# Attention with a token branch on one core: the tokens' second softmax product moved behind the next sample's y and V's first two blocks, its division moved behind the turning of the maximum

## The chip, the cores and the metric

The kernel runs on one core of one Trainium2 chip. The metric is the device time of one execution in microseconds. The kernel before takes 914.13 us, the median of three runs (914.01 to 916.65). All data are fp32.

A core has a matrix engine, TensorE (PE in the profile, with its weight loads shown apart as PEld), VectorE (DVE), ScalarE (ACT), GpSimd (POOL) and SyncE (SP), which issues most of the transfers here. Each engine runs its own list of instructions in order, and the lists meet at semaphores. Matmuls write to PSUM, a memory of eight banks, from which ScalarE and VectorE copy or add the results into SBUF.

## The reference

16 samples, each with 100 queries of width 640 and a context of 722 rows of width 384. The last 4 context rows are the "tokens" (`ca`), the other 718 are ordinary keys and values. 8 heads of width 80.

```python
query = hidden_states @ Wq
keyt = enc @ Wk
valt = enc @ Wv
hs = _mha(query, keyt, valt)                       # 100 queries on 718 keys
ca_q1 = jnp.einsum('btc,th->bch', ca, Wq_ca)
ca_q1 = ca_q1[:, indices, :]                       # 100 rows picked
ca_hs1 = _mha(ca_q1, residual, residual)           # the tokens' first attention, over x
ca_q2 = ca_hs1 @ Wq
ca_k2 = ca @ Wk_ca
ca_v2 = ca @ Wv_ca
ca_hs2 = _mha(ca_q2, ca_k2, ca_v2)                 # the tokens' second attention, 4 keys
out = (hs + ca_hs2) @ Wout + b_out + residual
```

## The kernel before

**The loop.** One pass of the loop `for b in range(B)` (L1410 on) handles sample b, and at the same time prepares sample b + 1. The order of the work is written out by hand: every engine executes its instructions in the order in which the program issues them. Samples 0 to 14 go through the branch `if b + 1 < B`; sample 15, the last, has a branch of its own.

In a pass, TensorE computes the scores of sample b in three parts (`scores(b, 0..2, ...)`, L688). Each part ends or begins with products of a 32-row shape (`others`) and of a 64-row shape (`heads`); the third part ends with the 32-row shape. ScalarE copies them to SBUF (L719, L725). VectorE keeps the running maximum in `most` (`larger(i)`, two element-wise maxima of about 1 us each, L1440). When all three parts are in, the class `Maximum` brings the maximum over the keys to every partition in steps: `top.go(1)` issues the first (a transpose, "turned", L760), the next reduces ("quad", L762), the next reduces again ("side" and "mx", L765 and L772), then it is spread and transposed back. After that the scores are reduced by it (`subtract`), exponentiated on ScalarE and multiplied with V (r_ps L1579 and a_ps L1597).

**The tokens' branch.** For sample b, `Second` makes `y` and `g` from x and a small matrix `m2` (`products()`: ten matmuls y_ps, L836, and a reduction g on VectorE, L845; `copy()`: ScalarE's copy of y out of PSUM into the one buffer `y_there`, L857). GpSimd then makes first scores `e1` out of g (`scores1`, L871 and L878); they pass a maximum and an exponential. In the next pass `softmax2()` multiplies the exponentials with y: 64 small matmuls with 32 output columns each into the bank z_ps (L898). One column of z_ps is the softmax's sum, so VectorE takes its reciprocal (L907) and multiplies (L909). `scores2()`, `softmax3()`, `spread2()` and `values2()` take it from there.

**V and K.** V of sample b and K of sample b + 1 are computed with 15 block products each (`V_PLAN`, `K_PLAN`), called by `vv.go(n)` and `kk.go(n)`, which issue the next n blocks. A V block is two accumulating targets of 320 columns, a K block two of 240. The letters A to E name the PSUM banks: the first blocks of V's plan are A, B, D, and K's too. A block's result is copied by ScalarE if it is the first for its place in the output (L418), else added by VectorE (L416).

**PSUM.** There are three pools: `ps2`, two pairs of banks (the third score part, then V's A and B); `psk`, two banks (K's A and B); and `ps1`, two single banks, of which y_ps, z_ps, V's D, E, C (one bank for each half) and K's D, E, C take turns. A new tile takes the bank that was let go first, and its first matmul waits until the last reader of the tile before is done with it.

So at the place of the change TensorE's order in samples 0 to 14 is: the third score part, z of sample b, y of sample b + 1, then V's A, B, D and K's A, B, D, and `scores2()` goes to the other engines behind that. In the pool `ps1` the takers are in turn z, y, V's D (two halves), K's D.

Of the kernel before, what the change touches and what calls it, by code (L numbers as in the profile page):

```python
# [14 lines left out]
B, S, H = 16, 100, 640  # L15
NH, D = 8, 80
# [26 lines left out]
HT = NH * T  # L43
# [44 lines left out]
def load_outputs(load, to, w):  # L88

    rows = w.rearrange("(c e k) n -> e c k n", e=2, k=D)  # L90
    for e in range(2):
        load(
            out=to[64 * e : 64 * e + 64, : HC - 1],
            in_=rows[e, :, FIRST[e] : FIRST[e] + 64].rearrange("c k n -> k c n"),
        )
        for c in range(HC - 1):
            at = 32 * c + 16 * e
            load(
                out=to[at : at + 16, HC - 1],
                in_=rows[e, c, 64:] if e == 0 else rows[e, c, : FIRST[1]],  # L100
            )
# [46 lines left out]
def kernel(  # L148
# [343 lines left out]
    def enc_sums(enc, part=slice(None)):  # L492

        at = lambda f: a_form(enc, f)
        raw = lambda u, c: a_raw(enc, u - 1, c - 1)
        sums = (
            (at(7), raw(2, 3), raw(3, 1), ALU.add),
            (at(11), raw(3, 2), raw(3, 3), ALU.add),
            (at(8), at(11), raw(2, 3), ALU.subtract),
            (at(10), raw(1, 3), at(11), ALU.subtract),  # L500
            (at(9), raw(2, 1), raw(2, 2), ALU.add),
            (at(2), raw(1, 1), at(9), ALU.subtract),
            (at(9), at(9), raw(3, 1), ALU.subtract),
            (at(5), raw(1, 1), raw(2, 1), ALU.subtract),
            (at(5), at(5), raw(2, 3), ALU.add),
            (at(11), raw(1, 3), raw(3, 3), ALU.subtract),
            (at(11), at(11), raw(3, 1), ALU.add),
            (at(4), at(2), at(10), ALU.add),
            (at(4), at(4), raw(1, 2), ALU.add),
        )  # L510
        begun = None
        for out, left, right, op in sums[part]:
            first = nc.gpsimd.tensor_tensor(out, left, right, op)  # L513
            begun = begun or first
        return begun
# [217 lines left out]
    def wait_for(ins, other):  # L733

        tc.add_manual_dep(
            ins.ins,
            other.ins.name,
            mybir.DependencyInfo(
                mybir.DependencyClass.Sync, mybir.DependencyReason.DATA
            ),  # L740
            reason="apart",
        )
# [49 lines left out]
    def load_m(b, behind=None):  # L792
        if b < 2:
            return lambda c: m_sb[c][:, b * HT : (b + 1) * HT]
        mb = small.tile([P, HC, HT], F32, tag="mb", name=f"mb_{b}")
        loaded = nc.sync.dma_start(
            out=mb, in_=m_d[:, :, b * HT : (b + 1) * HT].rearrange("c p n -> p c n")
        )
        if behind:
            wait_for(loaded, behind)  # L800
        return lambda c: mb[:, c]
# [13 lines left out]
    class Second:  # L815
# [77 lines left out]
        def softmax2(self):  # L893
            b = self.b
            z_ps = (psum1 if b + 1 < B else psumk)(f"z_ps_{b}")
            for h in range(NH):
                for lo, hi in QZ:
                    nc.tensor.matmul(  # L898
                        z_ps[lo:hi, h * (HT + 1) : (h + 1) * (HT + 1)],
                        e1[:S, h * S + lo : h * S + hi],  # L900
                        self.y[:, h, :],
                        start=True,
                        stop=True,
                    )
            z_v = z_ps[:S, : NH * (HT + 1)].rearrange("p (h k) -> p h k", h=NH)
            rz = small.tile([S, NH], F32, tag="rz", name=f"rz_{b}")
            nc.vector.reciprocal(rz.unsqueeze(2), z_v[:, :, HT:])  # L907
            z = small.tile([S, NH, HT], F32, tag="z", name=f"z_{b}")
            nc.vector.tensor_tensor(  # L909
                z, z_v[:, :, :HT], rz.unsqueeze(2).to_broadcast([S, NH, HT]), ALU.mult  # L910
            )
            self.z = z
# [88 lines left out]
    def again():  # L1001

        rows = wout.rearrange("(c e k) n -> e c k n", e=2, k=D)
        for e in range(2):
            nc.sync.dma_start(
                out=w_there[0][1][64 * e : 64 * e + 64],
                in_=rows[e, :2, FIRST[e] : FIRST[e] + 64, H // 2 :].rearrange(
                    "c k n -> k c n"
                ),
            )  # L1010
# [4 lines left out]
    def store(behind):  # L1015
        while held:
            r, xn = held.pop(0)
            lo, n = OC[r]
            stored = nc.sync.dma_start(
                out=out.rearrange("b s n -> (b s) n")[lo : lo + n], in_=xn[:n]  # L1020
            )
            wait_for(stored, behind)
# [367 lines left out]
    for c in range(HC):  # L1390
        for half in range(2):
            h = 2 * c + half
# [17 lines left out]
    for b in range(B):  # L1410
        p = b // 2
        e_in, now = enc, second
# [25 lines left out]
        def larger(i):  # L1438
            for u in range(2):
                most_now = nc.vector.tensor_tensor(  # L1440
                    most[:KN], most[:KN], st[i][:, u], ALU.max
                )
            return most_now
# [12 lines left out]
        vv = Values(b, e_in, V_PLAN if b + 1 < B else END_PLAN)  # L1456
        if b + 1 < B:
            kk = Keys(b + 1, enc)
        now.softmax2()
        if b + 1 < B:  # L1460
            second.products()
            second.copy()
        seen = larger(2)
        top = Maximum(most, f"{b}", True)

        if b + 1 < B:

            def both(n):
                vv.go(n)
                kk.go(n)  # L1470

            if waiting:
                wait_for(enc_sums(enc, LATE_SUMS), seen)
            if waiting:
                second.scores1(tokens=range(T - 1))
            else:
                second.scores1(seen)
            store(seen)
            if last:
                last.load(seen)  # L1480
            if b == B - 2:
                again()
            if b + 2 < B:
                m_next = load_m(b + 2, seen)
            if b == 1:
                load_outputs(nc.sync.dma_start, wout_sb, wout)
            top.go(3)
            both(3)
            now.scores2()
            top.go(1)  # L1490
            both(2)
            top.go()
            both(2)
            now.softmax3()
            if waiting:
                second.scores1(tokens=range(T - 1, T))
            if b + 2 < B:
                keys(m_next)
            both(1)
            now.spread2()  # L1500
            vv.go(2)
            kk.go(1)
            subtract(0)
            exponential(0)
            vv.go(1)
            less = subtract(1)
            if last:
                last.place(less)
                if last.b in PAIRED:
                    last.row_sums()  # L1510
                last.add_bias()
            if b == B - 2:
                mine.load(seen)
            now.values2()
            if b == B - 2:
                mine.add_bias()
            vv.go(1)
            kk.go(2)
            exponential(1)
            vv.go(1)  # L1520
            kk.go(2)
            both(1)
            both(1)
            if b == 1:
                nc.gpsimd.dma_start(out=bias, in_=bout[0].partition_broadcast(P))
            second_next, enc_next = loads()
            subtract(2)
            exponential(2)
            last_keys(b + 1, enc, b in (6, 7))
            if b + 2 < B:  # L1530
                enc_next = load_rest(b + 2, enc_next)
        else:
            last.place()
            mine.load(seen)
            top.go(3)
            vv.go(3)
            top.go(1)
            now.scores2()
            last.project_few(len(OC) - 2)
            last.project((0,), True, put=False)  # L1540
            top.go()
            now.softmax3()
            vv.go(1)
            now.spread2()
            vv.go(1)
            less = subtract(0)
            exponential(0)
            wait_for(subtract(2, nc.gpsimd), less)
            subtract(1, nc.gpsimd)
            mine.add_bias()  # L1550
            now.values2()
            vv.go(5)
            exponential(2)
            vv.go(1)
            exponential(1)
            vv.go(4)
            last.put()
# [109 lines left out]
```

## Time and profile before

| | |
|---|---|
| median of three runs | 914.13 us |
| the profiled execution, by the same clock as the runs | 915.1 us |
| its span, first to last instruction in the profile | 913.4 us |
| TensorE busy | 907.1 us, 99% |
| VectorE busy | 668.5 us, 73% |
| GpSimd busy | 619.4 us, 68% |
| ScalarE busy | 375.2 us, 41% |
| granted TensorE clock | 1.000 |

How to read the rows that follow: in the engine shares each engine has its busy time, its share of the span and the number of its instructions. A row of the waits names the waiting engine and line, what it waited for, the total in us, how often, and the longest. "issue" means that the profile shows nothing that was waited for. A row of the timeline begins with the start (us from the span's start) and the duration, then engine, line, operation, out<-in, the shape and the number of instructions that were merged; brackets give the engine's idle time ahead of it and what ended it. Matmuls overlap in the array: the start of a block and the start of the next one tell more than the duration.

### The profile page before, as it was taken

How to read it: one execution, taken by the hardware profiler on the slowest of the kernel's cores; microseconds unless marked ns; L12 is line 12 of the kernel's file. 1: busy time of each engine (PE TensorE's matmuls, PEld its weight loads, DVE VectorE, ACT ScalarE, POOL GpSimd, SP SyncE). 2: the span in 40 equal slices, each digit the busy share in tenths (PEclk: the TensorE clock that was granted, in tenths of full speed). 3: DMA queues.
4: the chain of work that ended last, by engine and by line, in shares of the span. 5: the costliest groups of instructions: out<-in, count | busy, mean ns of one | idle time of the engine just before them, and what ended most of it. 6: DMA issues, size and time to landing. Idle time of an engine off the chain costs nothing.

```text
span 913.4 us, 26025 instructions
## 1 busy us (share of the span) xinstructions
PE 907.1 (99%) x11127; PEld 758.2 (83%) x11127; DVE 668.5 (73%) x1121; ACT 375.2 (41%) x649; POOL 619.4 (68%) x653
## 2 busy tenths in 40 slices
PE   9999999999999999999999999999999999999998
PEld 7988889787887879878788888988888888887865
DVE  4899795979649796676957769588782888828773
ACT  1354534444334453443434434344541445424451
POOL 9664786677847788476674756755796567955635
PEclk9999999999999999999999999999999999999999
DMA  8604351141302303140221402304140151401313
GB/s 275 231 13 134 61 126 37 25 124 40 103 12 71 107 21 95 44 133 12 69 76 44 133 12 70 82 7 135 43 111 11 35 140 37 111 11 45 86 34 83
DMA packets 68060, 69.48 MB, mean 76 GB/s; under 512 B 25193, under 2 KB 61353, under 8 KB 67945
## 3 DMA queue, kind: packets, MB, share of 16 engines
q1 hardware_dynamic: 67016, 66.97, 27.1%
q8 instruction: 87, 1.43, 0.7%
q10 hardware_dynamic: 464, 0.52, 0.2%
q0 software_dynamic: 464, 0.34, 0.2%
q14 instruction: 29, 0.23, 0.1%
HBM read 62.14 MB, written 8.94 MB: 78 GB/s over the span
## 4 chain that ended last, share of the span: by engine, by line
PE 98%; POOL 1%; ACT 0%; DVE 0%; issue 0%; DVEq 0%; POOLq 0%
PE s_ps L688 12%; PE v_psA L445 11%; PE v_psB L445 9%; PE k_psA L476 8%; PE a_ps L1597 7%; PE q_ps L550 7%; PE k_psB L476 7%; PE kT_ps L601 5%; PE r_ps L1579 4%; PE v_psC L445 4%; PE kT_ps L576 3%; PE k_psC L476 3%; PE y_ps L836 2%; PE v_psD L445 2%; PE v_psE L445 2%; PE o_psy L1165 2%
## 5 line engine op out<-in xcount | busy, mean ns | idle before, releaser
L871 POOL TENSOR_TENSOR e<-ca,g 100x800 f32<-100x800 f32 x60 | 91.7, 1539 | 96.9 <-DVE most L1440 74.5
L445 PE MATMUL v_psA<-wv_sb,enc 128*120 128x320 f32 x384 | 119.5, 434 | 0.0
L513 POOL TENSOR_TENSOR enc<-enc 128x240 f32<-128x240 f32 x144 | 110.0, 773 | 8.0
L445 PE MATMUL v_psB<-wv_sb,enc 128*120 128x320 f32 x320 | 99.2, 432 | 0.0
L878 POOL TENSOR_TENSOR e<-e,e 100x800 f32<-100x800 f32 x45 | 92.2, 2048 | 3.5
L445 PEld LDWEIGHTS v_psA<-wv_sb,enc 128*120 128x120 f32 x384 | 69.0, 183 | 24.7 <-DVE vs L416 0.9
L1428 DVE TENSOR_TENSOR st<-st,over 120x1600 f32<-120x1600 f32 x46 | 88.7, 1929 | 0.0
L476 PE MATMUL k_psA<-enc,wk_sb 128*128 128x240 f32 x360 | 87.6, 366 | 0.0
L476 PEld LDWEIGHTS k_psA<-enc,wk_sb 128*128 128x128 f32 x360 | 68.4, 190 | 17.1
L445 PEld LDWEIGHTS v_psB<-wv_sb,enc 128*120 128x120 f32 x320 | 58.6, 183 | 23.4
L1436 ACT ACTIVATE st<-st 120x1600 f32<-120x1600 f32 x48 | 73.9, 1539 | 8.0 <-DVE st L1428 5.5
L1440 DVE TENSOR_TENSOR most<-most,st 120x800 f32<-120x800 f32 x64 | 63.5, 993 | 16.3 <-ACT st L719 15.1
L688 PE MATMUL s_ps<-qp,kT 64*56 64x100 f32 (+1 forms) x3072 | 73.5, 248 | 0.1
L476 PE MATMUL k_psB<-enc,wk_sb 128*128 128x240 f32 x300 | 73.0, 366 | 0.0
L688 PEld LDWEIGHTS s_ps<-qp,kT 64*64 64x64 f32 (+1 forms) x3072 | 67.0, 130 | 6.1 <-issue 4.2
L1449 DVE TENSOR_TENSOR most<-st 120x800 f32<-120x800 f32 x16 | 17.4, 1090 | 73.8 <-ACT st L725 73.8
L1597 PE MATMUL a_ps<-st,vs 120*64 120x100 f32 (+1 forms) x1536 | 69.5, 250 | 0.0
L550 PE MATMUL q_ps<-xT,wq_sb 128*128 128x200 f32 x400 | 69.1, 332 | 0.0
L1597 PEld LDWEIGHTS a_ps<-st,vs 120*64 120x64 f32 (+1 forms) x1536 | 66.4, 137 | 2.7 <-issue 2.7
L550 PEld LDWEIGHTS q_ps<-xT,wq_sb 128*128 128x128 f32 x400 | 68.0, 190 | 0.2
L418 ACT COPY vs<-v_psA 120x640 f32<-120x640 f32 x48 | 33.2, 692 | 83.7 <-PE v_psA L445 83.7
L725 ACT COPY st<-s_ps 120x800 f32<-120x800 f32 x64 | 49.7, 829 | 43.2 <-PE s_ps L688 43.1
(187 smaller groups left out, 1874.7 us busy)
## 6 DMA issues: line engine op xcount, KB each, us to landing
pb<-p_d SPq DMA_DIRECT2D x32, 400.0 KB
enc<-in_enct SPq DMA_DIRECT2D x30, 240.0 KB
enc<-in_enct SPq DMA_DIRECT2D x15, 360.0 KB
xT<-in_xt SPq DMA_DIRECT2D x8, 500.0 KB
rest<-in_enct SPq DMA_DIRECT2D x31, 120.0 KB
xn<-in_x SPq DMA_DIRECT2D x11, 320.0 KB
wide_d<-p_d SPq DMA_DIRECT2D x16, 200.0 KB
pb<-wide_d SPq DMA_DIRECT2D x16, 200.0 KB
```

The source lines that it names most:

```text
L445: nc.tensor.matmul(at[0][j][:KN, : H // 2], a_form(self.enc, f)[:, j * KN : (j + 1) * KN], wv_sb[:, W_AT[f]], start=first, stop=last, skip ...
L476: nc.tensor.matmul(at[:, i * KT : (i + 1) * KT], wk_sb[:, W_AT[f], i], a_form(self.enc, f), start=(first and i == 0), stop=last, skip_grou ...
L513: first = nc.gpsimd.tensor_tensor(out, left, right, op)
L550: nc.tensor.matmul(q_ps[:, : 2 * S].rearrange("p (j s) -> p j s", j=2), wq_sb[:, c, n * P : (n + 1) * P], xT[:, :, c, :], start=(c == 0), ...
L688: nc.tensor.matmul(s_ps[bank][keys, 256 * a + lo : 256 * a + lo + rhs.shape[-1]], kT[rows, c, u, j * KN + keys.start : j * KN + keys.stop] ...
L725: nc.scalar.copy(st[:, :, 4 * i * S : 4 * (i + 1) * S].rearrange("p a (r q) -> p r a q", r=2), pairs[i][:n].rearrange("p r (a q) -> p r a ...
L871: first = engine.tensor_tensor(to, self.ca[:, t, :].unsqueeze(1).to_broadcast([S, NH, S]), g[:, :, t].unsqueeze(2).to_broadcast([S, NH, S] ...
L878: engine.tensor_tensor(e, e, to, ALU.add)
L1428: return engine.tensor_tensor(st[i], st[i], top.over[:KN].unsqueeze(1).to_broadcast([KN, 2, ROWS]), ALU.subtract,)
L1436: nc.scalar.activation(st[i], st[i], AF.Exp, scale=SCALE)
L1440: most_now = nc.vector.tensor_tensor(most[:KN], most[:KN], st[i][:, u], ALU.max)
L1597: nc.tensor.matmul(wides[64 * e : 64 * e + 64, h // 2], slot(i, h, FIRST[e], 64), st[i // 2][: KEYS[i], i % 2, PLACE[h] * S : (PLACE[h] + ...
```

## The change

In samples 0 to 14 the product of `softmax2()` (z) is issued behind the next sample's `products()` (y) and the first two blocks of V (A and B), where it was issued ahead of them. ScalarE's copy of y is issued behind z, as z still reads the old y out of the one buffer. The reciprocal and the multiplication by it become a method of their own, `divide2()`, issued on VectorE behind the last `larger(2)` and behind the first step of the maximum (the turning); before they stood ahead of `larger(2)`. The blocks that followed are issued as K's A and B, then V's D, then K's D. In sample 15 `divide2()` follows `softmax2()` directly, which is the order of before.

```diff
                         start=True,
                         stop=True,
                     )
-            z_v = z_ps[:S, : NH * (HT + 1)].rearrange("p (h k) -> p h k", h=NH)
+            self.z_ps = z_ps
+
+        def divide2(self):
+            b = self.b
+            z_v = self.z_ps[:S, : NH * (HT + 1)].rearrange("p (h k) -> p h k", h=NH)
             rz = small.tile([S, NH], F32, tag="rz", name=f"rz_{b}")
             nc.vector.reciprocal(rz.unsqueeze(2), z_v[:, :, HT:])
...
         if b + 1 < B:
             kk = Keys(b + 1, enc)
-        now.softmax2()
         if b + 1 < B:
             second.products()
+            vv.go(2)
+            now.softmax2()
             second.copy()
+        else:
+            now.softmax2()
+            now.divide2()
         seen = larger(2)
         top = Maximum(most, f"{b}", True)
...
-            top.go(3)
-            both(3)
+            top.go(1)
+            now.divide2()
+            top.go(2)
+            kk.go(2)
+            vv.go(1)
+            kk.go(1)
             now.scores2()
             top.go(1)
             both(2)
```

`both(n)` stands for `vv.go(n)` followed by `kk.go(n)`.

## The prediction

> **What bounds the kernel now.** I read the page's engine shares first, then the chain that ended last, then the waits of TensorE's weight loads, and last the timeline around the moved product.
>
> ```profile
> PE 907.1 (99%) x11127; PEld 758.2 (83%) x11127; DVE 668.5 (73%) x1121; ACT 375.2 (41%) x649; POOL 619.4 (68%) x653
> ...
> PE 98%; POOL 1%; ACT 0%; DVE 0%; issue 0%; DVEq 0%; POOLq 0%
> ...
> PEld r_ps L1579 <- issue: 5.0, 15, 0.4
> PEld s_ps L688 <- issue: 4.2, 17, 0.3
> PEld z_ps L898 <- issue: 3.9, 15, 0.5
> ...
> PEld z_ps L898 <- ACT e L891: 0.4, 1, 0.4
> ```
>
> TensorE (PE) is busy for 907.1 of 913.4 us and makes 98% of the chain. So a microsecond on another engine is worth nothing unless it makes a matmul wait, and a microsecond in which TensorE waits is lost at full price. The matmuls stay the same in number and shape. What can change is the time between them. The last four rows are the weight loads' idle time: almost all of it stands at "issue", with no data named, and z, the product that is moved, has 3.9 us of it in 15 of its 16 instances.
>
> The edit acts in samples 0 to 14. In sample 15 the product and its division follow each other as before. This is the stretch of sample 2 (start, duration; x counts the instructions):
>
> ```profile
> 157.20 0.95 PE L688 MATMUL s_ps<-qz,kT 32*120 32x200 f32 x16
> 158.08 0.75 PE L898 MATMUL z_ps<-y,e 100*32 100x33 f32 x64
> 158.76 1.21 PE L836 MATMUL y_ps<-m,xT 128*100 128x96 f32 x10
> 159.80 1.26 PE L445 MATMUL v_psA<-wv_sb,enc 128*120 128x320 f32 x4
> 160.90 1.24 PE L445 MATMUL v_psB<-wv_sb,enc 128*120 128x320 f32 x4
> 161.98 1.24 PE L445 MATMUL v_psD<-wv_sb,enc 128*120 128x320 f32 x4
> 163.05 0.97 PE L476 MATMUL k_psA<-enc,wk_sb 128*128 128x240 f32 x4
> 163.86 0.97 PE L476 MATMUL k_psB<-enc,wk_sb 128*128 128x240 f32 x4
> 164.67 0.97 PE L476 MATMUL k_psD<-enc,wk_sb 128*128 128x240 f32 x4
> ```
>
> From start to start: z 0.68, y 1.04, vA 1.10, vB, vD 1.08 each, a K block 0.81. TensorE waits for none of them. The new order is y, vA, vB, z, kA, kB, vD, kD.
>
> **The change part by part.** *The start of y in z's place.* The scores' last products (32-row shape) are followed by 0.24 us of idle weight loads before z:
>
> ```profile
> 158.08 0.64 PEld L898 LDWEIGHTS z_ps<-y,e 100*32 100x32 f32 x64 [0.24 <-issue]
> ...
> 191.86 2.05 PEld L1579 LDWEIGHTS r_ps<-st,vs 120*32 120x32 f32 x96 [0.30 <-issue]
> ...
> 189.34 0.57 PE L601 MATMUL kT_ps<-rest,wk 128*128 128x240 f32 x2
> 189.74 1.78 PE L601 MATMUL kT_ps<-enc,wk 128*128 128x240 f32 x8
> 191.36 0.57 PE L601 MATMUL kT_ps<-rest,wk 128*128 128x240 f32 x2
> 191.86 2.27 PE L1579 MATMUL r_ps<-st,vs 120*32 120x100 f32 x96
> ```
>
> Such idle time stands wherever the tile shape changes, here too before r (0.30), whose operands were long there. So y will find it as z did, and starts at 158.08. If it did not, it could win 0.24 at most, and the next step takes that away again.
>
> *vA moves up by z's 0.68 us.* It writes the pair of banks from which ScalarE (ACT) copies the last scores:
>
> ```profile
> L725 ACT COPY st<-s_ps 120x800 f32<-120x800 f32 x64 | 49.7, 829 | 43.2 <-PE s_ps L688 43.1
> ...
> 158.24 1.55 ACT L725 COPY st<-s_ps 120x800 f32<-120x800 f32 x2 [0.91 <-PE s_ps L688]
> ...
> 162.77 0.91 ACT L418 COPY vs<-v_psD 120x320 f32<-120x320 f32 x2
> 164.06 0.56 ACT L418 COPY kT<-k_psA 128x480 f32<-128x480 f32 x1 [0.39 <-PE k_psA L476]
> 164.87 0.56 ACT L418 COPY kT<-k_psB 128x480 f32<-128x480 f32 x1 [0.25 <-PE k_psB L476]
> ```
>
> The first row is their group on the page: a copy takes 829 ns on average, and two overlap a little: the first pair is free near 159.07, the second at 159.79. vA would come at 158.08 + 1.04 = 159.12. With some 0.05 us for a semaphore (the k_psE rows below) it can go at about 159.12 to 159.20: between 0 and 0.08 us lost, I take 0.03 as the copy is all but done. vB follows at 160.25, long after the second copy. If vA has the second pair, it waits to 159.84, 0.7 us per sample. I put that aside because in another sample the copies ran later and vA did not:
>
> ```profile
> 599.18 1.55 ACT L725 COPY st<-s_ps 120x800 f32<-120x800 f32 x2 [1.19 <-PE s_ps L688]
> ...
> 600.46 1.26 PE L445 MATMUL v_psA<-wv_sb,enc 128*120 128x320 f32 x4
> ```
>
> There the second copy ended at 600.73, and vA had begun at 600.46: it has the first pair. This also says why y's start cannot pay: before 159.07 vA may not write.
>
> *One more change of shape.* Before, the array goes from 32-row scores to z (32 columns) and from z to the full shapes; now from scores to full, from full to z, from z to full. Full to 32 columns costs what kT to r costs: the last two kT matmuls take 191.86 - 191.36 = 0.50 us where the like pair took 189.74 - 189.34 = 0.40, so 0.10. Before, y was the first full-shape product behind z; now y follows the scores, which were a change of shape all along, and kA follows z. What that costs kA is seen in the last sample, where a V block follows z:
>
> ```profile
> 871.89 1.34 PE L445 MATMUL v_psD<-wv_sb,enc 128*120 128x320 f32 x4
> 873.06 1.24 PE L445 MATMUL v_psA<-wv_sb,enc 128*120 128x320 f32 x4
> 874.14 1.24 PE L445 MATMUL v_psB<-wv_sb,enc 128*120 128x320 f32 x4
> ```
>
> 1.17 us where the next block takes 1.08: 0.10 with rounding. Together 0.20; the bounds are 0 (covered by the engine's own overlap) and 0.30 + 0.10, by r's idle time. z then starts at 160.25 + 1.08 + 0.10 = 161.43, kA at 162.11, kB at 163.02, vD at 163.83, kD would be due at 164.91.
>
> The Trainium skill, TensorEngine Tiling (Array Packing), Key Properties, says that a change of tiling mode drains TensorE, which speaks against this edit: three drains for two. The trace agrees as to the idle time (0.24 and 0.30 us); at 0.30 us for the third drain alone the 15 samples would lose 4.5 us, by the starts of the matmuls they lose 1.5 us there.
>
> *kD behind vD.* D blocks use a pool of two single banks that go round: y, z, vD's halves, kD. kD takes the bank of vD's first half, as it did before; then kA and kB (1.62 us) lay between and hid ScalarE's copy out of it. Now nothing does. That such a bank is waited for, and the price, stands once in sample 0, where kE needs a bank of vE:
>
> ```profile
> 69.40 0.70 PEld L476 LDWEIGHTS k_psE<-enc,wk_sb 128*128 128x128 f32 x4 [0.26 <-DVE vs L416]
> ...
> 68.89 0.85 DVE L416 TENSOR_TENSOR vs<-v_psE,vs 120x320 f32<-120x320 f32 x2
> ...
> 68.54 0.97 PE L476 MATMUL k_psA<-enc,wk_sb 128*128 128x240 f32 x4
> 69.40 1.08 PE L476 MATMUL k_psE<-enc,wk_sb 128*128 128x240 f32 x4
> 70.31 1.24 PE L445 MATMUL v_psB<-wv_sb,enc 128*120 128x320 f32 x4
> ```
>
> The weight load idled 0.26 us, of which some 0.01 is usual; the two blocks took 0.86 and 0.91 for 0.81 each, 0.15 in all, so about 0.10 of an idle load is absorbed. The load began about 0.05 after the first of the two additions (69.35 by the halves of 0.85). Now kD: vD's first half ends at 163.83 + 0.27 + 0.43 = 164.53 (a quarter of the block, and the rest of one matmul's duration); ScalarE is at kB's copy until 163.02 + 1.01 + 0.56 = 164.59, then copies the half in 0.43 (0.91 for two, overlapping): 165.01. kD's load may go at 165.06; it would have gone at 164.65, a quarter of a block before 164.91. Idle 0.41, less the 0.10: 0.31 us. The bounds: 0, if the bank is another; 0.74, if it is that of the second half, copied 0.43 later.
>
> The Trainium skill, TensorE: Matmul & The Clock Gate, Step-by-step, says that the weight load is pulled ahead of running matmuls. If it passed the wait too, kD would lose only 165.06 - 164.91 = 0.15 us, and the sum below would be 5.6 us. The k_psE row speaks against that here: it is the load that stands idle for the bank.
>
> *y's copy, the division, the maximum.* They cost nothing by these covers. y's copy (0.37) now waits for z to end at 162.18, and runs to some 162.6; vD, which takes y's bank, starts at 163.83. On VectorE (DVE):
>
> ```profile
> 159.30 0.20 DVE L907 RECIPROCAL rz<-z_ps 100x8 f32<-100x8 f32 x1
> 159.53 0.42 DVE L909 TENSOR_TENSOR z<-z_ps,rz 100x256 f32<-100x256 f32 x1
> ...
> 160.18 2.01 DVE L1440 TENSOR_TENSOR most<-most,st 120x800 f32<-120x800 f32 x2
> 162.22 1.01 DVE L760 STREAM_TRANSPOSE turned<-most 128x800 f32<-128x800 f32 x1
> ```
>
> Without the division in front, the last maximum waits for the scores' copy only and runs 159.85 to 161.86, the turning ends near 162.9, z is there by 162.65, and reciprocal and product end near 163.6. vD's second half takes that bank at 163.83 + 0.54, so the cover is 0.8 us. Behind it stand the maximum's reduction, scores2 and the V and K additions, 0.4 us later than before (163.6 against 162.22 + 1.01 = 163.23), while TensorE is 0.5 us later: those who wait for them lose no slack. GpSimd's scores of the next sample, released by the last maximum, start 0.3 us earlier, off the path. No DMA is issued elsewhere, and SP's queue and POOL's keep their order.
>
> *The sum.* 0.03 + 0.20 + 0.31 = 0.54 us for each of 15 samples, 8.1 us, less 0.1 in sample 0, where z waited for its exponentials (the 0.4 row, against 0.24 to 0.26 usual) and y now fills that. The profiled execution took 915.1 us (span 913.4 and 1.7 around it), so it would take 923.1. The median of the runs is 914.13, 1.0 below it: 922.1, I say 922.
>
> **The rivals.** *Bank wait hidden.* kD's copy is in time, or the bank another; only shape and vA remain, 0.23 x 15 = 3.5 us: 917.5. For it: between kB's and vD's copies ScalarE has little else. Against it: the copy cannot begin before the half is done, and kD is due 0.4 us after that.
>
> *No change.* The array overlaps the extra change of shape and the copy as well: 914. For it speaks that y to vA costs only 0.02 to 0.03 (1.10 for 1.08); against it the 0.10 of kT to r, in every such place.
>
> *Faster.* The 0.24 before z is a wait for something that z alone needs, and goes as z is moved behind 3 us of work, while the new place costs nothing. This decides if z's entry at vB shows no idle time and vA's bank is free by 158.9. It gives 15 x 0.24 = 3.6 us: 910.5. Against it: the s_ps row has the same idle at 17 places (4.2 / 17 = 0.25), where scores follow scores, and vA's bank is free at 159.07.
>
> *The later bank, or a longer copy.* kD waits for the second half, 0.74 instead of 0.31: 0.97 x 15 = 14.5 us, 928.7.
>
> **How the numbers follow.** The forecast has 0.63, the hidden bank wait 0.15, no change 0.08, faster 0.06, the later bank 0.08. A measurement of this kernel can tell about 0.3%, 2.7 us, from no change: 911.4 to 916.9. The hidden wait lies just above that bound and I give a third of it to "within". Faster 0.06, within 0.13, slower 0.81. The range leaves out the faster case, most of the later bank and a part of no change: 915.5 to 927. Its upper end has the whole idle of 0.41, 0.08 for vA and 0.30 + 0.10 at the shapes: 0.89 x 15 = 13.4 above 914, rounded down.
>
> **What would show it.** In the changed trace: idle weight loads before y of about 0.24 and before z of about 0.3; kA's block behind z 0.9 instead of 0.81; rows of k_psD waiting for ACT vs L418, 15 times about 0.4 us, or none if the forecast is wrong in its largest term; v_psA waiting for ACT st at most 0.1 each. TensorE's busy time would stay within a few us of 907 while the span grows. The prediction falls if kD starts right behind vD, or if the idle before y is gone and vA starts earlier than 1.04 us after the scores.

## The result, and the profile after

The changed kernel takes 920.0 us (median of five runs, 919.66 to 920.32), the kernel before 914.14 (914.01 to 916.65). The ratio is 1.0051, with a 95% interval of 1.0038 to 1.0064: slower by half a per cent. The forecast was 922, in a range of 915.5 to 927.

The first lines are the engine shares and the chain of the changed kernel, then the waits of its weight loads (total in us, times, longest).

```profile
PE 912.1 (99%) x11127; PEld 755.0 (82%) x11127; DVE 671.1 (73%) x1121; ACT 377.3 (41%) x649; POOL 634.1 (69%) x653
...
PE 96%; DMA 2%; POOL 1%; SPq 1%; DVE 0%; ACT 0%; issue 0%; ACTq 0%; DVEq 0%; POOLq 0%
...
PEld k_psD L476 <- ACT vs L418: 7.4, 15, 0.5
PEld z_ps L898 <- issue: 6.5, 15, 0.4
...
PEld y_ps L836 <- issue: 3.7, 15, 0.2
```

The number of matmuls is the same, TensorE is still the bound, and 4.6 us more stand in its span (918.0 for 913.4). The waits name the places. The largest is new: 15 times, once in each changed sample, K's D block waits for ScalarE's copy of V's D block. z's idle time at "issue" grew from 3.9 us (14 starts of z, and 0.5 for a single stop in its midst, told of below) to 6.5, and y took over the 0.24 us per sample that z had behind the scores. The page's busy time does not set this apart: it grew by 5.0 us, about as much as the span, as a matmul that is stretched by a late weight load counts as busy (kD's block 1.08 us for 0.97). So the sign that busy time would stay near 907 us while the span grows is of no use here; the waits and the starts of the matmuls tell. The 2% of DMA in the chain stand in the first 25 us, before the part that was changed (see the last section).

The same stretch in the changed kernel, sample 7, on TensorE:

```profile
431.74 1.21 PE L836 MATMUL y_ps<-m,xT 128*100 128x96 f32 x10
432.78 1.33 PE L445 MATMUL v_psA<-wv_sb,enc 128*120 128x320 f32 x4
433.95 1.24 PE L445 MATMUL v_psB<-wv_sb,enc 128*120 128x320 f32 x4
435.12 0.75 PE L898 MATMUL z_ps<-y,e 100*32 100x33 f32 x64
435.79 1.08 PE L476 MATMUL k_psA<-enc,wk_sb 128*128 128x240 f32 x4
436.71 0.97 PE L476 MATMUL k_psB<-enc,wk_sb 128*128 128x240 f32 x4
437.52 1.24 PE L445 MATMUL v_psD<-wv_sb,enc 128*120 128x320 f32 x4
438.74 1.08 PE L476 MATMUL k_psD<-enc,wk_sb 128*128 128x240 f32 x4
439.65 1.24 PE L445 MATMUL v_psA<-wv_sb,enc 128*120 128x320 f32 x4
```

and its weight loads at the four places that the prediction named:

```profile
431.74 1.04 PEld L836 LDWEIGHTS y_ps<-m,xT 128*100 128x100 f32 x10 [0.24 <-issue]
432.77 0.82 PEld L445 LDWEIGHTS v_psA<-wv_sb,enc 128*120 128x120 f32 x4
...
435.12 0.64 PEld L898 LDWEIGHTS z_ps<-y,e 100*32 100x32 f32 x64 [0.45 <-issue]
...
438.73 0.70 PEld L476 LDWEIGHTS k_psD<-enc,wk_sb 128*128 128x128 f32 x4 [0.49 <-ACT vs L418]
```

From y's start to the start of the second A block of V it takes 439.65 - 431.74 = 7.91 us. Before, the same eight pieces took 165.48 - 158.08 = 7.40. So a sample loses 0.51 us. From start to start, before and after: vA 1.10 and 1.17; vB 1.08 and 1.17; K's A behind z 0.81 and 0.92; vD and kD together 1.89 and 2.13; y, z and kB are as before. In full nanoseconds the four differences are 70, 94, 104 and 244, the same in all later samples to a few.

15 x 0.51 = 7.7 us, and the medians differ by 5.9. The difference is taken up in the section on the steps.

### The profile page after: what moved, and what is told of

Read it like the earlier page. It is cut to its first block, busy times and chain, and to the rows that moved or that the text cites. A ratio compares the mean times of both kernels' runs of the same rounds, so it can differ in the third digit from the quotient of the medians.

```text
span 918.0 us, 26018 instructions
## 1 busy us (share of the span) xinstructions
PE 912.1 (99%) x11127; PEld 755.0 (82%) x11127; DVE 671.1 (73%) x1121; ACT 377.3 (41%) x649; POOL 634.1 (69%) x653
## 4 chain that ended last, share of the span: by engine, by line
PE 96%; DMA 2%; POOL 1%; SPq 1%; DVE 0%; ACT 0%; issue 0%; ACTq 0%; DVEq 0%; POOLq 0%
PE s_ps L688 12%; PE v_psA L445 11%; PE v_psB L445 9%; PE k_psA L476 8%; PE a_ps L1609 7%; PE q_ps L550 7%; PE k_psB L476 7%; PE kT_ps L601 5%; PE r_ps L1591 4%; PE v_psC L445 4%; PE k_psC L476 3%; PE y_ps L836 2%; PE v_psD L445 2%; PE o_psy L1169 2%; PE v_psE L445 2%; PE k_psD L476 2%
## 5 line engine op out<-in xcount | busy, mean ns | idle before, releaser
L688 PE MATMUL s_ps<-qp,kT 64*64 64x100 f32 (+1 forms) x3072 | 73.1, 248 | 0.0
```

What stands on the lines that cost most here:

```text
L688: nc.tensor.matmul(s_ps[bank][keys, 256 * a + lo : 256 * a + lo + rhs.shape[-1]], kT[rows, c, u, j * KN + keys.start : j * KN + keys.stop] ...
```

## The experiments

The kernel before was run beside each of them. Its median was 914.82 us beside the first four, 914.61 beside the next two and 914.21 beside the last two.

### The kernel before once more

No edit.

> The kernel before, unchanged, timed against itself, for a second profile of it. In the steady part the changed kernel loses 0.51 us in each of 15 samples, 7.7 us, but its profiled execution is only 4.6 us and its median 5.9 us longer. Theory A (chance): the missing 2 to 3 us are not of the change. The first profile of before had a slower first 10 us (matmuls at half speed until 9.9 us, until 6 us in the changed kernel's profile: 1.6 us) and three single stalls (0.55, 0.21 and 0.44 us near 373, 487 and 647 us) that come at other places or not at all in a second profile; the steady part is the same to 0.05 us per sample. Theory B (of the program): the same three stalls and the same slow start come again, to 0.1 us. Either way the ratio is 1.000 within 0.002.

Measured: 914.55 us, ratio 0.9995 (0.9987 to 1.0004). The steady part of a sample is the same to 0.01 us. Both theories hold in part. The slow start did not come again: it differs by 1.0 us from the first profile. Single stalls of the matmuls came again, 1.0 us in sum against 1.2: one at the same place, z of sample 6, with 0.22 us (0.55 in the first profile), and four at other places, of 0.13 to 0.24 us in the scores. They are shown below, where they matter.

### kD one block later

```diff
             kk.go(2)
             vv.go(1)
-            kk.go(1)
             now.scores2()
             top.go(1)
-            both(2)
+            vv.go(1)
+            kk.go(1)
+            vv.go(1)
+            kk.go(2)
```

> The changed kernel, with K's D block issued one V block later: kA, kB, vD, then V's next A block, then kD. The theory (kD waits for ScalarE's copy of vD's first half, 0.24 us per sample, and nothing else takes its place): no row of k_psD waiting for ACT, 15 x 0.24 = 3.7 us won against the changed kernel, so about 916.3 us. The rival (the wait is only where the loss shows; TensorE would wait for VectorE or ScalarE a little later anyway): about 920, with new wait rows of v_psA, v_psE or k_psE.

Measured: 924.96 us, ratio to before 1.0108 (1.0093 to 1.0123), 5 us more than the changed kernel (3.6 of them in the loop over the samples, by the two profiles, the rest ahead of it). The theory's first half held: the wait of k_psD is gone from the rows. Its second half fell, and the rival's new waits are there. The waits of the weight loads in this run:

```profile
PEld k_psE L476 <- DVE vs L416: 6.3, 15, 0.4
PEld v_psE L445 <- ACT kT L418: 6.1, 15, 0.7
```

V's E block waits for a K copy of ScalarE. ScalarE's and the weight loads' timeline of one sample says why:

```profile
444.82 0.23 ACT L933 ACTIVATE e<-e 100x32 f32<-100x32 f32 x1 [1.87 <-DVE e L930]
444.96 1.71 ACT L782 COPY spread<-mx 64x800 f32<-64x800 f32 x2
446.70 0.56 ACT L418 COPY kT<-k_psD 128x480 f32<-128x480 f32 x1
...
443.14 0.86 PEld L476 LDWEIGHTS k_psD<-enc,wk_sb 128*128 128x128 f32 x4
444.01 0.92 PEld L445 LDWEIGHTS v_psB<-wv_sb,enc 128*120 128x120 f32 x4
...
447.31 0.33 PEld L445 LDWEIGHTS v_psE<-wv_sb,enc 128*120 128x120 f32 x2 [0.21 <-ACT kT L418]
```

kD's matmuls were through by about 444.3, yet its copy ran from 446.70: in ScalarE's list it stood behind the exponential of scores2 and the two spreading copies, as the edit had put kD's block behind them. vE's second half takes kD's bank and started only when the copy was done, at 447.31. So this run did not show whether a later kD pays; it showed that a block is moved on two engines at once.

### y ahead of z, and nothing else

```diff
-        now.softmax2()
         if b + 1 < B:
             second.products()
+        now.softmax2()
+        if b + 1 < B:
             second.copy()
```

> The kernel before with one edit: y is issued ahead of z, and y's copy behind z. V's blocks, the division and all the rest stay in place. The theory (one more change of the tile shape in every sample costs about 0.20 us, of which 0.09 stands ahead of z and 0.10 in the block behind it): 15 x 0.20 = 3.0 us lost against before, about 917.1; idle weight loads before y of 0.24 and before z of about 0.3. The rival (the shape's change is free, the changed kernel loses by its waits for banks alone): 914.1. No waits for ACT at v_psA or k_psD under either.

Measured: 916.53 us, ratio 1.0019 (1.0010 to 1.0027), 1.7 us above before. The rival is out. TensorE in sample 7 of this run:

```profile
431.94 1.21 PE L836 MATMUL y_ps<-m,xT 128*100 128x96 f32 x10
433.07 0.75 PE L898 MATMUL z_ps<-y,e 100*32 100x33 f32 x64
433.75 1.34 PE L445 MATMUL v_psA<-wv_sb,enc 128*120 128x320 f32 x4
434.92 1.24 PE L445 MATMUL v_psB<-wv_sb,enc 128*120 128x320 f32 x4
```

y takes 1.13 (1.04 before), z 0.68 (as before), vA 1.17 (1.10 before). That is 0.17 us per sample and 2.5 us in all, 0.8 more than the medians show: the extra change of shape costs 0.09 ahead of z and 0.07 in vA behind it, as vA behind y already had 0.02. No wait of v_psA or k_psD for ScalarE stands among the rows. One expected sign did not come, the idle load of about 0.3 before z:

```profile
431.94 1.04 PEld L836 LDWEIGHTS y_ps<-m,xT 128*100 128x100 f32 x10 [0.24 <-issue]
433.07 0.64 PEld L898 LDWEIGHTS z_ps<-y,e 100*32 100x32 f32 x64
```

z's load stands idle for 433.07 - (431.94 + 1.04) = 0.09 us here and for 0.45 in the changed kernel, and the path pays 0.09 both times.

### kD directly behind vD, and nothing else

```diff
             top.go(3)
-            both(3)
+            vv.go(2)
+            kk.go(2)
+            vv.go(1)
+            kk.go(1)
             now.scores2()
```

> The kernel before with one edit: the blocks behind vB are issued as kA, kB, vD, kD instead of vD, kA, kB, kD. z, y and the division stay in place. The theory (the bank of vD's first half has no cover): 15 rows of k_psD waiting for ACT vs L418, 0.4 to 0.5 us each, 0.24 us per sample on the path, 15 x 0.24 = 3.7 us lost, about 917.8. The rival (the wait comes from the change's later copies on ScalarE, not from the order of the blocks): 914.1 and no such rows.

Measured: 918.13 us, ratio 1.0029 (1.0017 to 1.0042). The waits of the weight loads:

```profile
PEld k_psD L476 <- ACT vs L418: 7.4, 15, 0.5
```

It is the changed kernel's row to the digit, with z, y and the division where they were before. vD and kD together take 2.13 us, 0.24 more, in every sample, 3.7 us in all. The order of the blocks alone makes this wait; the rival is out.

### The division as well

The edit is the one above, and `divide2()` as in the changed kernel, issued behind the first step of the maximum.

```diff
...
-            top.go(3)
-            both(3)
+            top.go(1)
+            now.divide2()
+            top.go(2)
+            vv.go(2)
+            kk.go(2)
+            vv.go(1)
+            kk.go(1)
```

> The kernel before with the blocks behind vB in the order kA, kB, vD, kD, and with the division moved behind the turning of the maximum; z and y stay in place. Against the run with the order of the blocks alone this shows the division's price. The theory (the division is off TensorE's path; but z's bank is let go later, and vD's second half, due some 5.8 us behind z's start, finds it free at about 5.85): 0 to 0.1 us per sample more than the order of the blocks alone, 917.8 to 919.3. The rival (the later maximum makes the exponentials late, and TensorE waits at r_ps): rows of r_ps waiting for ACT st in many samples, some 0.3 us each, 922.

Measured: 918.24 us, ratio 1.0038 (1.0025 to 1.0050), 0.1 us from the run without the moved division. r_ps does not wait more than before. There is one small new row:

```profile
PEld k_psE L476 <- DVE vs L416: 1.5, 5, 0.4
```

kE waits in five samples for VectorE's addition of vE, which stands behind the later division; 0.3 us of idle load and about 0.2 us on the path each time, 1 us in all. The two medians hide this microsecond: the profile of the run above lost about 1 us more in its first 54 us, ahead of the first z (a stop shown in the last section). In the changed kernel no such row stands among the waits, so there the division costs nothing that its rows show.

### Both waits for banks covered, first try

```diff
             second.products()
+            kk.go(1)
             vv.go(2)
             now.softmax2()
...
-            kk.go(2)
-            vv.go(1)
-            kk.go(1)
+            kk.go(1)
+            vv.go(1)
             now.scores2()
             top.go(1)
-            both(2)
+            vv.go(1)
+            kk.go(1)
+            vv.go(1)
+            kk.go(2)
```

> The changed kernel with both waits for banks covered: K's A block is issued between y and vA (so the scores' copy is done when vA comes), and kD one V block later. z stays behind vB. The order is y, kA, vA, vB, z, kB, vD, vA, kD. The theory (0.07 for vA, 0.24 for kD, the rest of 0.20 is the change of tile shape and stays): 15 x 0.20 = 3.0 us above before, about 917.1, with no rows of v_psA or k_psD waiting for ACT. The rival (the change of shape is free when blocks are long enough): 914.1. A second rival (the waits move to the next blocks): 919 or more.

Measured: 932.23 us, ratio 1.0194 (1.0179 to 1.0208). The second rival came true. The wait is that of the first move of kD, vE for ScalarE's copy of kD, and longer; in both orders kD's block stands behind scores2 and the spreading:

```profile
PEld v_psE L445 <- ACT kT L418: 14.3, 15, 1.1
```

### kD later, with its copy ahead in ScalarE's list

```diff
             kk.go(2)
-            vv.go(1)
+            vv.go(2)
             kk.go(1)
             now.scores2()
             top.go(1)
-            both(2)
+            vv.go(1)
+            kk.go(2)
```

> The changed kernel with kD one V block later (kA, kB, vD, vA, kD), as in the run that moved kD alone, but with vA and kD issued ahead of scores2 and the maximum's spreading, so that ScalarE's copy of kD stands ahead of their exponential and their two spreading copies in its queue. The theory (that run lost its gain since kD's copy waited in ScalarE's queue behind them, and vE needs kD's bank): no waits of k_psD, none of v_psE for ACT kT, 0.24 x 15 = 3.7 us below the changed kernel, about 916.3. The rival (a later kD makes vE late in any order): the v_psE waits stay, 920 or more. A second rival (VectorE, which now adds vA ahead of scores2, makes the next blocks late): rows of k_psE waiting for DVE vs, 918 to 920.

Measured: 918.53 us, ratio 1.0040 (1.0027 to 1.0052). TensorE's blocks stand in the same order as in the run that took 924.96 us; only the issue of scores2 and of the spreading stands behind kD's block. kD's copy now runs ahead of the exponential:

```profile
441.27 0.56 ACT L418 COPY kT<-k_psD 128x480 f32<-128x480 f32 x1 [1.46 <-PE k_psD L476]
443.30 0.23 ACT L933 ACTIVATE e<-e 100x32 f32<-100x32 f32 x1 [1.48 <-DVE e L930]
443.44 1.71 ACT L782 COPY spread<-mx 64x800 f32<-64x800 f32 x2
```

The waits of k_psD and v_psE are gone. The second rival has a small part: k_psE waits for VectorE ten times, 1.8 us of idle loads, which cost the path some 0.06 us each and 0.2 in sample 0. A sample is 0.24 us shorter than in the changed kernel where kE does not wait, and 0.19 where it does, 2.9 us over the loop. Its five times lie at 916.9 to 917.3 and at 918.5 to 918.7; the profile is of the upper group and had a first stretch about 2 us slower than the changed kernel's.

### Both covered, copies ahead

```diff
             second.products()
+            kk.go(1)
             vv.go(2)
             now.softmax2()
...
-            kk.go(2)
-            vv.go(1)
+            kk.go(1)
+            vv.go(2)
             kk.go(1)
             now.scores2()
             top.go(1)
-            both(2)
+            vv.go(1)
+            kk.go(2)
```

> The same with K's A block between y and vA as well, so that both waits for banks are covered and only the change of shape is left of the three prices: y, kA, vA, vB, z, kB, vD, vA, kD. The theory: 0.07 x 15 = 1.1 us below the run before it, about 915.2, that is the kernel before plus 0.20 x 15 = 3.0 us, less about 1 us of single stalls that the profiles of kernels with z directly behind the scores have, and those with z behind V's blocks have not, less their scatter. The rival (z behind V's blocks costs by itself more than the change of shape): 918 or more with no waits for banks in the rows.

Measured: 915.61 us, ratio 1.0013 (1.0004 to 1.0022), 4.4 us below the changed kernel. TensorE in sample 7:

```profile
429.96 1.21 PE L836 MATMUL y_ps<-m,xT 128*100 128x96 f32 x10
431.00 1.00 PE L476 MATMUL k_psA<-enc,wk_sb 128*128 128x240 f32 x4
431.84 1.24 PE L445 MATMUL v_psA<-wv_sb,enc 128*120 128x320 f32 x4
432.92 1.24 PE L445 MATMUL v_psB<-wv_sb,enc 128*120 128x320 f32 x4
434.08 0.75 PE L898 MATMUL z_ps<-y,e 100*32 100x33 f32 x64
434.76 1.08 PE L476 MATMUL k_psB<-enc,wk_sb 128*128 128x240 f32 x4
435.68 1.24 PE L445 MATMUL v_psD<-wv_sb,enc 128*120 128x320 f32 x4
436.75 1.24 PE L445 MATMUL v_psA<-wv_sb,enc 128*120 128x320 f32 x4
437.83 0.97 PE L476 MATMUL k_psD<-enc,wk_sb 128*128 128x240 f32 x4
```

vA is back to 1.08, vD and the next A to 1.07 and 1.08, and what is left is vB ahead of z (1.17 in full nanoseconds) and kB behind it (0.91): 0.20 us per sample above before, as the change of shape had been priced: 3.0 us, less the 1 us of stalls told of below, where the median is 1.4 us above before. It is the fastest kernel with z behind V's blocks, and not faster than before.

## Why the prediction was right, step by step

**The bound.** As stated: no instruction of another engine was worth anything but by a wait of TensorE, and every wait of TensorE was paid in full.

**The start of y.** Foretold 0.24 us of idle loads ahead of y, measured 0.24 (the y_ps row). Nothing was won there. The reason given, that such idle time stands wherever the tile shape changes, is too wide: behind z the load of y stood idle for only 0.04 us before (158.08 + 0.64 = 158.72, y at 158.76), and in the run with y ahead of z the load of z for 0.09.

**vA on the scores' bank.** Foretold 0 to 0.08, taken 0.03; measured 0.07. The load began at 432.77, some 0.06 later than the usual one (before, 0.08 ahead of its matmul, now 0.01), so it was no longer hidden. ScalarE's first copy began at 431.89; with the 0.83 us that one takes it ended at 432.72, and the load followed 0.05 later, the time that the prediction had read from the k_psE rows. The wait is too short for a row of its own. With K's A block between, the 0.07 went; that is the support by experiment.

**The extra change of shape.** Foretold 0.20; measured 0.094 ahead of z and 0.104 behind it. The run with y ahead of z alone and the last run both show it without the waits, at 0.17 (with vA behind) and 0.20. The idle load ahead of z is 0.45 us behind a V block and 0.09 behind y, and the path pays 0.09 both times: behind vB the rest lies beside the block's last matmuls, which run to 433.95 + 1.24 = 435.19. So the idle load is not the price, the starts of the matmuls are. The Trainium skill, TensorEngine Tiling (Array Packing), Key Properties, says that a change of tiling mode drains TensorE; by the starts, the extra change costs 0.2 us here for both sides together. The part behind z need not be a cost of the change as such: kD pays the same 0.104 us behind its bank wait (0.914 us for 0.810), with no change of shape ahead of it. In both places the block's load starts with its matmul (435.79 and 435.79; 438.73 and 438.74) and not 0.20 us ahead as behind a K block before.

**kD on vD's bank.** Foretold 0.31 us; measured 0.244. The cause is as foretold, and the run with this order alone shows it by itself. The idle load was right too: 0.41 was foretold, the row has 0.49, and 0.09 of that is the usual pause behind a V block, as the weight loads of the kernel before show:

```profile
161.71 0.99 PEld L445 LDWEIGHTS v_psD<-wv_sb,enc 128*120 128x120 f32 x4
162.79 0.86 PEld L476 LDWEIGHTS k_psA<-enc,wk_sb 128*128 128x128 f32 x4
...
164.47 0.80 PEld L476 LDWEIGHTS k_psD<-enc,wk_sb 128*128 128x128 f32 x4
```

(161.71 + 0.99 = 162.70, and the next load at 162.79.) The step that was off is the absorption: 0.10 by the single kE event, 0.16 here (0.40 - 0.244). A reason can be read from these rows, though no run shows it by itself: a load behind a V block goes 0.26 us ahead of its matmul (162.79 for 163.05), behind a K block, as kE's did, 0.20 (164.47 for 164.67). What a late load may lose without harm is of the size of that lead, so it grows by 0.06. Seen by the starts, the 0.244 is 0.14 of a later start (vD 1.217 us for 1.077) and the 0.104 in kD's own block. The rival in which the load passes the wait would have had the 0.15 of the later start alone.

**The division and the maximum.** Foretold at nothing, and it is so in the changed kernel: no wait for VectorE came in with it. With z left in its old place and kD behind vD it is not quite nothing (about 0.2 us in five samples).

**The sum.** Foretold 0.54 per sample, measured 0.51. The terms' errors (0.04 too low at vA, 0.07 too high at kD) nearly cancel. But 15 x 0.51 = 7.7 us is more than the 5.9 between the medians. Sample 0 loses 0.36 less than the others, where 0.1 was foretold: z's late start there cost 0.21 in the first profile of before, and kE's wait, from which the prediction took its price, 0.15; neither stands in the changed kernel's sample 0. (In the second profile of before z lost the 0.36 alone.) About 1 us is a gain that the prediction did not have: the single stalls. These rows are z of sample 6 in the first profile of the kernel before, in the run with kD behind vD, and in the changed kernel:

```profile
373.20 0.55 PE L898 MATMUL z_ps<-y,e 100*32 100x33 f32 x41
374.11 0.39 PE L898 MATMUL z_ps<-y,e 100*32 100x33 f32 x23 [0.36 <-issue]
```

```profile
374.41 0.60 PE L898 MATMUL z_ps<-y,e 100*32 100x33 f32 x44
375.40 0.38 PE L898 MATMUL z_ps<-y,e 100*32 100x33 f32 x20 [0.40 <-issue]
```

```profile
377.80 0.75 PE L898 MATMUL z_ps<-y,e 100*32 100x33 f32 x64
```

In sample 6 TensorE stops once in the midst of z, with nothing waited for that the profile shows, in all four profiles with z directly behind the scores (0.22 to 0.63 us); in the changed kernel it does not. Other such stalls stand in the scores, in z or in y, in other samples from profile to profile. Summed over the samples they make 1.2 and 1.0 us in the two profiles of before and 0.9 to 1.0 us in each of the three runs that keep z ahead of V's blocks; the changed kernel and the four runs with z behind V's first blocks have none above 0.02 us. So the new place seems to have a gain, some seven times smaller than its price. What remains, 0.3 to 0.5 us, is within the scatter of the start, last section. What the stalls are (the profile has only "issue"), and why the new order is without them, also in the scores, was not tried and stays open. The forecast of 922 came within 2 us of the 920.0 with the right terms; that the errors of vA and kD have opposite signs was luck.

**The rivals.** "Bank wait hidden" fell by the k_psD row. "No change" and "faster" fell by the same and by vB's 1.17. "The later bank" would have made kD wait for the second half, 0.74; 0.244 excludes it.

## What to carry to other kernels

When one engine is the bound, cost a reordering by the starts of its instructions: count the changes of tile shape along the new order, and for every buffer that goes round ask what lay between its reader and its next writer before, and what lies there now. A block that is moved on one engine is moved in the list of every engine that serves it: the same order of matmuls took 924.96 us with kD's copy behind an exponential and 918.53 with the copy ahead of it. An order that removes one wait is only proven by the rows of the next user of the same buffer.

## What the runs showed of the hardware that was not expected

**The first 10 us differ by up to 2 us between executions of kernels that are the same there.** The busy time and the number of matmuls that ended up in the stretch from 6 to 8 us, in the first profile of before, in the changed kernel's, and in that of the run with kD's copy ahead:

```profile
6.00:8.00 2.00, 2.00 (x6) 1.00 0.91 234
```

```profile
6.00:8.00 2.00, 1.91 (x12) 1.00 0.67 169
```

```profile
6.00:8.00 2.00, 1.79 (x5) 1.00 0.86 221
```

The columns are the stretch, busy TensorE with its matmuls, the granted clock, the DMA share and GB/s. In two of them TensorE did half as many matmuls in the same busy time, at about 0.40 us from start to start for 0.20. The column of the granted clock says 1.00 in all. The Trainium skill, TensorE: Matmul & The Clock Gate, describes such a start in Part 1: The HAM clock gate: a half-rate array until some 3.4 us of activity have passed in a window that runs freely, so that the moment varies from run to run. The doubling agrees with that, and so does the kind of scatter. Its size does not: the Trainium skill, in the same part, has the moment vary by about half a microsecond, and here full rate is reached by 5.85 us in the changed kernel and at 9.86 in the first profile of before. The profile's clock column does not show it, and no run here proves it.

The slow start may be behind the two groups of times in the run with kD's copy ahead, whose profile is of the upper group. It does not explain the upper of the two groups, 2 us apart, in the run with kD behind vD (915.95 to 916.32 and 918.13 to 918.6). The profile there is of the upper group too, and has 12 matmuls from 6 to 8 us; but TensorE stands still for 2.0 us ahead of the block m_ps, at 24 us, and the chain of that profile has a transfer of V's weights which lands at 21.96 (first a row of the waits, then one of the chain, start and duration):

```profile
PEld m_ps L1354 <- issue: 2.0, 1, 2.0
...
11.07 10.89 DMA wv_sb<-in_wv
```

In the changed kernel, too, the chain reaches the start of m_ps, at 24.73 us, through a transfer of weights (12.77 us, landed at 24.59). So the start of this kernel has two limits that lie close together, the matmuls' rate and the arrival of weights, and both bound what single runs can tell here.

**An extra change of tile shape between full-shape blocks costs 0.09 us ahead of the small product and 0.10 us in the block behind it, while the waits show an idle load of 0.45.** In the changed kernel and in the last run both were the same to 0.01 us in every changed sample. The 0.10 is also what kD pays behind its bank wait, where the shape stays the same.

**TensorE's stalls in runs of very short matmuls**, about 1 us per execution, came in all five profiles with z ahead of V's blocks; the five with z behind them have none above 0.02 us. The cause is open.
